# Two edits to a hybrid state-space, attention and feed-forward kernel: B's rows through DRAM with a reordered first group, and a softmax transpose moved to VectorE and the DMA queue

## The chip, the cores and the metric

The kernel runs on one core of a Trainium2 chip, in float32 apart from a few bf16 helpers. The metric is the device time of one execution in microseconds (us). Three runs of the kernel before took 2170.24, 2170.4 and 2171.72 us; the median is 2170.4 us.

A core has five engines that run side by side, each through its own list of instructions in order: TensorE (PE, matrix products, with PEld for its weight loads), VectorE (DVE), ScalarE (ACT), GpSimd (POOL) and SyncE (SP), which here only issues DMAs. They wait for one another through semaphores.

## The reference

The input `x` has shape (16, 256, 128): 16 sequences, 256 tokens, width 128. Four residual blocks follow one another, each on a layer norm of `x`:

```python
x = x + ssm(_layernorm(x), ...)      # selective state space, E = 256 channels, N = 16 states
x = x + ffn(_layernorm(x), ...)      # two layers: windowed attention and a gated MLP
x = x + attn_b(_layernorm(x), W)     # power attention, 16 heads
x = x + ffn(_layernorm(x), ...)      # the same two layers again
```

What matters of the state space block is its recurrence over time, for each of the 16 states:

```python
delta = softplus(xs @ wd1.T @ wd2.T + wd2_b);  Bm = xs @ wb.T;  Cm = xs @ wc.T
h = exp(d_l[:, :, None] * A) * h + (d_l * x_l)[:, :, None] * b_l[:, None, :]
y_l = einsum('ben,bn->be', h, c_l)
```

What matters of a feed-forward layer is its local attention. A sequence has windows of 64 tokens, 8 heads of width 64; a query sees itself and the 64 keys before it:

```python
mask = (i < j) | (i > j + WINDOW) | (j == -1)
attn = softmax(where(mask, -max, einsum('bhwid,bhwjd->bhwij', bq, bk)))
out = einsum('bhwij,bhwjd->bhwid', attn, bv)
```

## The kernel before

**Order.** Each engine is wrapped in `Pinned` (line 78), so that its instructions run in the order in which the program issues them. Every steady loop is written as a list of words: a word is a step, its arguments, and after the colon its lag, the number of iterations by which it runs behind. `wt00.1:4` is the step `wt` for tile 0, half 0, of the second sequence of the group that entered four iterations ago. The order of the words is the order of the instructions on every engine.

**State space block.** The 16 sequences go in 8 groups of 2, so a group has C = 512 columns (2 x 256 tokens), and the 256 channels are 2 halves of 128 partitions. For each group and each of the 16 states n (a "tick") the kernel needs: `decay`, ACT's exponentials; `spread`, a DMA that gives every partition the row of B for state n (tile `bb`); `inputs`, which multiplies delta times x (`dx`) by `bb` into `bx`; `scan`, VectorE's recurrence; `products`, times C, on VectorE or, for three states, on GpSimd; and `add`, TensorE's accumulation. B's rows are computed by `reps`: its weights `wrep` hold each of the 16 columns of B eight times, so the product fills all 128 partitions, `reps_out` copies it to SBUF, and `spread` reads the eight copies of a row and sends each to 16 partitions. The prologue (from `neg_a` and `cw` on) treats group 0 outside the steady list: conv weights `cw`, normed rows, `turn`, convolution into `xe_ps`, `rows`, `reps`, `steps_in`, and then `steps` (delta and dx) and `inputs` for ticks 0 and 1, these on GpSimd.

**Feed-forward blocks.** One runs after the state space block and one after the power block, overlapping it at both ends. A block treats 32 units (2 layers x 16 sequences) as 16 groups of 2, with seven iterations in flight. A sequence is 2 tiles (t = 0, 1) of 128 queries. Per tile: `mask` and `scores` into a pair of PSUM banks, `maxima` and `less_maximum` on VectorE, `exponentials` on ACT, `sums` on VectorE, `weights_of` on GpSimd. This leaves the softmax weights `pr`, 128 queries on partitions by (2 x 4 heads) x 128 keys. The product with V needs keys on the partitions, so `turn_weights` (`wt`) transposes 4 heads at a time on TensorE against the identity, into a PSUM bank, and `turned_weights` (`wc`) copies it to `prT` by ACT. `weigh` (`we`) multiplies V by `prT`. The second tile sees 3 windows of keys and is treated as two halves; in the first tile the queries 0 to 127 see only keys 0 to 127, of which those after the query and those more than 64 before it carry weight 0. `values_out` and `mixed` issue DMAs on SP: two for shifted copies of V, three for the token shift before the MLP. All of a block's tiles lie in one array `mem`, which an `Arena` divides (`FFN_LATE` lists the second part).

**Power block.** It is untouched. Its `spread` reads rows from DRAM (tile `pngd`) and broadcasts them to 128 partitions.

Of the kernel before, what the change touches and what calls it, by code (L numbers as in the profile page):

```python
# [12 lines left out]
F32 = mybir.dt.float32  # L13
# [7 lines left out]
P = 128  # L21
D = 128
L = 256
E = 256
NST = 16
# [20 lines left out]
def kernel(ctx: ExitStack, tc: tile.TileContext, io, out: bass.AP):  # L46
# [72 lines left out]
    def ssm_block(fill):  # L119
        es = ExitStack()  # L120
        w = es.enter_context(tc.tile_pool(name="ssm_w", bufs=1))
        prep = es.enter_context(tc.tile_pool(name="ssm_prep", bufs=1))
        work = es.enter_context(tc.tile_pool(name="ssm_work", bufs=4))
        ps_m = es.enter_context(tc.tile_pool(name="ssm_psm", bufs=1, space=PSUM))
        ps_a = es.enter_context(tc.tile_pool(name="ssm_psa", bufs=1, space=PSUM))
# [23 lines left out]
        wall = w.tile([P, NE, P], F32, name="wall")  # L149

        NR = P // NST
        wrep = w.tile([P, NE, P], F32, name="wrep")
        for e in range(NE):
            part = slice(e * P, (e + 1) * P)
            nc.sync.dma_start(quarters(wall[:, e])[:, :, 0, :], io["wd1T"][part].rearrange("p (j n) -> p j n", j=NQ))
            nc.sync.dma_start(
                quarters(wall[:, e])[:, :, 1, :], io["wcT"][part].unsqueeze(1).to_broadcast([P, NQ, NST])
            )
            nc.sync.dma_start(
                wrep[:, e].rearrange("p (j n) -> p j n", j=NR),  # L160
                io["wbT"][part].unsqueeze(1).to_broadcast([P, NR, NST]),
            )
        wd2T = w.tile([P, E], F32, name="wd2T")
# [119 lines left out]
        def reps(h, q, at=None):  # L283

            q["pb"] = bank([P, C], f"reps_ps_{h}") if at is None else at
            for e in range(NE):
                pe.matmul(q["pb"], wrep[:, e, :], q["xs"][:, e, :], start=(e == 0), stop=(e == NE - 1))

        def reps_out(h, q):
            q["reps"] = prep.tile([P, C], F32, name=f"reps_{h}", tag="reps", bufs=2)  # L290
            act.copy(q["reps"], q.pop("pb"))

# [45 lines left out]

        def steps(h, q, e):
            if e == 0:  # L340
                q["dx"] = prep.tile([P, NE, C], F32, name=f"dx_{h}", tag="dx", bufs=2)
            delta = q["delta"][:, e, :]
            pool.tensor_add(delta, delta, q["av"][:, e, :])
            pool.tensor_mul(q["dx"][:, e, :], delta, q["xs"][:, e, :])

# [5 lines left out]
        def spread(i):  # L351

            bb = live["bb", i] = work.tile([P, C], F32, name=f"bb_{i}", tag="bb")
            src = groups[i // NST]["reps"][i % NST :: NST, :].unsqueeze(1).to_broadcast([NR, NST, C])
            sp.dma_start(bb, src)
# [9 lines left out]

        def inputs(i):
            bx = live["bx", i] = work.tile([P, NE, C], F32, name=f"bx_{i}", tag="bx")
            bb = live.pop(("bb", i)).unsqueeze(1).to_broadcast([P, NE, C])
            pool.tensor_mul(bx, groups[i // NST]["dx"], bb)

# [71 lines left out]
        py = ps_y.tile([P, NE, C], F32, name="cw_ps", tag="y")  # L442
        pts = [py[:, e].rearrange("p (k m) -> p k m", k=DCONV) for e in range(NE)]
        for e in range(NE):
            dve.tensor_tensor(
                tap[:, e], pi[:, e].unsqueeze(1).to_broadcast([P, DCONV, P]),
                conv_w[:, e].unsqueeze(2).to_broadcast([P, DCONV, P]), ALU.mult,
            )
            for k in range(DCONV):
                pe.transpose(pts[e][:, k, :], tap[:, e, k, :], ident)  # L450
            act.copy(cw[:, :, e * P : (e + 1) * P], pts[e])

        sel = w.tile([3 * QW, NST, P], BF16, name="sel")
# [16 lines left out]
        q, r = groups[0], groups[1]  # L470
        normed_rows(0, q)
        turn(0, q)
        turned(0, q)
        more_weights()
# [9 lines left out]
        rows_out(0, q)  # L484
        pb = ps_c.tile([P, C], F32, name="reps_ps_0", tag="c")
        reps(0, q, pb)
# [7 lines left out]
        for e in range(NE):  # L494
            steps_out(0, q, e)
            logs(0, q, e)
            steps(0, q, e)
        for i in range(2):
# [3 lines left out]
        third(0, q)  # L502
        for i in range(2):
            inputs(i)
        rows_of_c(0)
# [36 lines left out]
        for i in range(NG + max(lag for _, _, lag, _ in parts)):  # L542
            for step, more, lag, name in parts:
                h = i - lag
                if (name, h) in done or not (0 <= h < NG or (step is silus and h == NG)):
                    continue
                if step in by_state:
                    step(h * NST + more[0])
                elif step is silus and h == NG:
                    silus(NG, None)  # L550
                elif step is conv:
                    e, half = more
                    conv(h, groups[h], e, range(2 * half, 2 * half + 2))
                else:
                    step(h, groups[h], *more)

                if step is scan and fill is not None and more[0] % 3 == 0:
                    next(fill, None)
# [172 lines left out]

    FFN_LATE = [("rn", 32, 2), ("qkT", 2048, 2), ("vx", 1536, 4), ("pr", 1024, 3), ("prT", 1024, 2), ("oT", 512, 2)]
    FFN_LATE += [("mx", 8, 4), ("rl", 8, 4), ("shifted0", 512, 1), ("shifted1", 512, 1), ("hn", 512, 1)]
# [3 lines left out]
    def ffn_block(k, fw, store, shared):  # L737
# [19 lines left out]
        hTs = [sb.tile([P, L], F32, f"f{k}_hT{i}", f"hT{i}") for i in range(2)]  # L757
        shifted = [sb.tile([P, GT, D], F32, f"f{k}_shifted{i}", f"shifted{i}") for i in range(2)]
        first = []

# [155 lines left out]
        def mask(n, q, t):  # L916
# [4 lines left out]
            if not first:  # L921
# [3 lines left out]
                for h in shifted:  # L925
                    pool.memset(h[:1, 0::2, HD:], 0.0)
            act.copy(
                psim.rearrange("p r h k -> p (r h) k"), fw["bands"][t].unsqueeze(1).to_broadcast([P, 2 * NP, P])
# [49 lines left out]


        def turned_weights(n, q, t, r):  # L980
            if r == 0:
# [3 lines left out]
        def weigh(n, q, t):  # L985

            prT, vx = q.pop(("prT", t)), q["vx"]
            po = bank(q, ("po", t), [P, NP, P], f"f{k}_po_{n}_{t}")
            for p in range(NP):
                for w in range(t + 1):  # L990
                    qs = slice(w * WINDOW, (w + 1) * WINDOW) if t else slice(0, P)
                    for r in range(2):
                        pe.matmul(
                            po[r * DH : (r + 1) * DH, p, qs], vx[:, 2 - w if t else 0, 2 * p + r, :],
                            prT[:, r, p, qs], start=True, stop=True,
                        )
            sb.free(prT)
            sb.free(vx, 2)
# [93 lines left out]
        def unit_sum(g, q):  # L1092
# [12 lines left out]
            nw=newton, no=normed, t=turn, tc=turned, k=mask, s=scores, mx=maxima, lm=less_maximum,  # L1105
            e=exponentials, su=sums, wo=weights_of, wt=turn_weights, wc=turned_weights, we=weigh,
            oc=weighed, mi=mix, ma=mixed, Us=unit_stats, Uf=unit_factors, Un=unit_norm, Ut=unit_turn,
# [3 lines left out]
        period = """  # L1111
            ns.0:0 Uf:5 p00.0:2 e1.1:4 ma0.0:4 ro01.0:2 t11.0:3 s0.0:3 tc11.0:3 ro11.1:3 oc1.0:4
            v0.0:2 sq00.0:2 su1.1:4 ra11.1:3 Ud0:6 vc0.0:2 Un:5 mx0.0:3 t10.0:3 wt00.1:4 ss00.0:2
            tc10.0:3 wt01.1:4 lm0.0:3 wc00.1:4 Ud1:6 ra01.0:2 wc01.1:4 i.1:3 mi1.0:4 n.0:1 wo1.1:4
            p11.0:2 ma1.0:4 Ua:6 v1.0:2 ro00.0:2 nw.1:3 sq11.0:2 k1.0:3 p10.0:2 ss01.0:2 ra00.0:2
            vc1.0:2 p00.1:2 ro11.0:2 Ut:5 no00.1:3 s1.0:3 Uc:5 no01.1:3 e0.0:3 we0.1:4 mx1.0:3
            ra11.0:2 sq10.0:2 nf.1:1 oc0.1:4 ut.0:1 wt10.1:4 ss10.0:2 wt11.1:4 lm1.0:3 wc10.1:4
            Ur10:5 uc.0:1 wc11.1:4 Ur11:5 ss11.0:2 e1.0:3 ro10.0:2 b.0:2 we1.1:4 no11.1:3 k0.1:3
            su0.0:3 ra10.0:2 t00.1:3 oc1.1:4 v0.1:2 tc00.1:3 su1.0:3 no10.1:3 t01.1:3 vc0.1:2
            p01.1:2 sq00.1:2 wo0.0:3 Ur12:5 tc01.1:3 ss00.1:2 sq01.1:2 ro00.1:2 mi0.1:4 i.0:2 Ug:5  # L1120
            wo1.0:3 s0.1:3 ma0.1:4 ro01.1:2 mi1.1:4 nw.0:2 Ur01:5 ma1.1:4 mx0.1:3 ra00.1:2 p10.1:2
            ss01.1:2 t10.1:3 Ub:5 sq10.1:2 Um1:5 t11.1:3 tc10.1:3 v1.1:2 lm0.1:3 tc11.1:3 no00.0:2
            wt00.0:3 vc1.1:2 wt01.0:3 no01.0:2 ss10.1:2 ns.1:0 wc00.0:3 p01.0:1 ro10.1:2 wc01.0:3
            no11.0:2 Ur00:5 k1.1:3 ra01.1:2 wt11.0:3 Um0:5 e0.1:3 wt10.0:3 Us:4 we0.0:3 n.1:1
            ra10.1:2 wc10.0:3 sq01.0:1 s1.1:3 oc0.0:3 su0.1:3 wc11.0:3 ut.1:1 p11.1:2 mx1.1:3
            wo0.1:3 Ur02:5 uc.1:1 Um2:5 t00.0:2 t01.0:2 no10.0:2 tc00.0:2 lm1.1:3 we1.0:3 sq11.1:2
            tc01.0:2 nf.0:0 mi0.0:3 ss11.1:2 k0.0:2 b.1:2
        """
# [436 lines left out]
```

## Time and profile before

| what | us |
|---|---|
| median of the runs | 2170.4 |
| the profiled execution | 2171.14 |
| its span, first to last instruction | 2169.3 |
| TensorE busy | 2028.6 |
| VectorE busy | 1841.5 |
| ScalarE busy | 1706.5 |
| GpSimd busy | 1899.4 |

The span divides into the state space block (to about 490 us), the first feed-forward block (to about 1150), the power block (to about 1500) and the second feed-forward block. The granted TensorE clock is 0.981 on average. A feed-forward block has a pulse: its gate step (three activations and two table loads on ACT, once a group) is at 605.0, 644.9, 684.0, 723.0 us and so on, 39.08 us apart for ten intervals in a row, then 38.87, 30.70 and 25.46 us as it drains; the second block repeats these to 0.1 us. The duration of an instruction in these listings includes its latency; what instructions in a row cost their engine is the distance between their starts.

### The profile page before, as it was taken

Reading aid. Unit: us, or ns where it says so; the run is one execution under the profiler, and the core shown is the slowest. Engines: PE = TensorE matmul, PEld = TensorE weight load, DVE = VectorE, ACT = ScalarE, POOL = GpSimd, SP = SyncE. Lnnn points to the kernel's source line nnn. Section 1 sums busy time; section 2 is a strip of 40 time slices with the busy share of each in tenths; the row PEclk is TensorE's granted clock in tenths of the full one; section 3 lists DMA queues with packets and bytes.
Section 4 is the critical chain, followed back from the end, with each engine's and each line's share of the span. In section 5 each row is a group of like instructions: output and inputs, shape, how many; then the busy total and the mean of one; then the engine's idle time right before and its main releaser. Section 6 shows DMA issues by size and latency. Waiting matters only on the chain.

```text
span 2169.3 us, 44282 instructions
## 1 busy us (share of the span) xinstructions
PE 2028.6 (94%) x16172; PEld 1331.3 (61%) x16174; DVE 1841.5 (85%) x3285; ACT 1706.5 (79%) x2879; POOL 1899.4 (88%) x2183
## 2 busy tenths in 40 slices
PE   5999999877999999999998999998899999999997
PEld 2344444334667777777765777775567777777775
DVE  2999999997989888888856999997988888888873
ACT  4777777746888887887865999997788887878874
POOL 7999999967999888888967999996999988888993
PEclk8999999998999999999997999999999999999998
DMA  4333333321001110111103323230010111101110
GB/s 93 97 83 81 98 80 79 79 52 24 18 22 23 23 23 17 23 23 23 23 11 118 101 98 119 84 114 9 21 23 17 23 23 23 23 16 33 28 28 23
DMA packets 97350, 104.21 MB, mean 48 GB/s; under 512 B 51458, under 2 KB 63596, under 8 KB 97132
## 3 DMA queue, kind: packets, MB, share of 16 engines
q1 hardware_dynamic: 96444, 101.22, 18.4%
q8 instruction: 128, 2.10, 0.4%
q14 instruction: 90, 0.74, 0.1%
q10 hardware_dynamic: 688, 0.15, 0.1%
HBM read 40.28 MB, written 2.36 MB: 20 GB/s over the span
## 4 chain that ended last, share of the span: by engine, by line
PE 54%; POOL 17%; DVE 9%; ACT 9%; issue 7%; DMA 2%; SPq 2%; POOLq 0%; DVEq 0%; ACTq 0%
PE bank L88 44%; POOL bx L88 7%; PE pair L88 7%; POOL mem L88 7%; DVE mem L88 6%; ACT mem L88 5%; DVE hs L88 2%; ACT pair L88 2%; SPq L88 2%; POOL hs L88 1%; PE xe_ps L88 1%; DMA mem<-u_all 1%; DMA bb<-reps 1%; POOL sf L88 1%; PE y_ps L88 1%
## 5 line engine op out<-in xcount | busy, mean ns | idle before, releaser
L88 POOL TENSOR_TENSOR mem<-mem 128x256 f32<-128x256 f32 (+5 forms) x1328 | 1156.7, 901 | 88.4 <-DVE mem L88 66.2
L88 ACT COPY mem<-bank 128x512 f32<-128x512 f32 (+4 forms) x1152 | 590.7, 556 | 147.6 <-PE bank L88 142.0
L88 PEld LDWEIGHTS bank<-ident,mem 128*128 128x128 f32 x3104 | 353.5, 141 | 171.2 <-issue 109.4
L88 PE MATMUL bank<-ident,mem 128*128 128x128 f32 x3104 | 426.0, 277 | 15.1 <-POOL mem L88 10.2
L88 PE MATMUL bank<-wqkv,mem 128*128 128x512 f32 x768 | 385.8, 607 | 1.8 <-ACT mem L88 1.8
L88 DVE TENSOR_REDUCE mem<-mem 128x8 f32<-128x512 f32 (+1 forms) x384 | 325.6, 849 | 9.8 <-ACT mem L88 9.4
L88 DVE TENSOR_TENSOR mem<-bank,rope 128x1024 f32<-128x1024 f32 x256 | 308.8, 1216 | 24.1 <-POOL mem L88 15.8
L88 DVE TENSOR_TENSOR_SCAN hs<-a,bx 128x1024 f32<-128x1024 f32 x128 | 291.4, 2281 | 38.6 <-POOL bx L88 35.5
L88 POOL TENSOR_TENSOR bx<-dx,bb 128x1024 f32<-128x1024 f32 x128 | 298.5, 2357 | 4.0 <-DVE hs L88 3.3
L88 ACT ACTIVATE mem<-mem 128x1024 f32<-128x1024 f32 (+2 forms) x384 | 280.2, 735 | 24.4 <-DVE mem L88 16.3
L88 PE MATMUL pair<-mem 64*64 64x128 f32 (+2 forms) x4096 | 256.7, 296 | 22.0 <-DVE mem L88 13.5
L88 PE MATMUL y_ps<-hs,ident 128*128 128x512 f32 x512 | 242.8, 599 | 11.4 <-DVE hs L88 6.7
L88 PEld LDWEIGHTS pair<-mem 64*64 64x64 f32 (+2 forms) x4096 | 194.9, 160 | 74.2 <-issue 26.2
L88 ACT ACTIVATE a<-delta,neg_a 128x510 f32<-128x510 f32 x256 | 176.0, 689 | 79.1 <-DVE hs L88 73.5
L88 ACT ACTIVATE mem<-bank 128x512 f32<-128x512 f32 (+1 forms) x272 | 160.6, 591 | 62.9 <-PE bank L88 58.6
L88 PE MATMUL bank<-mem 128*64 128x64 f32 (+2 forms) x4608 | 203.3, 255 | 5.3 <-ACT mem L88 2.9
L88 PE MATMUL bank<-mem,w 128*128 128x512 f32 x384 | 193.5, 603 | 3.8 <-ACT mem L88 3.8
L88 PEld LDWEIGHTS bank<-mem 128*64 128x64 f32 (+1 forms) x4608 | 156.8, 128 | 64.3 <-issue 30.1
L88 PEld LDWEIGHTS y_ps<-hs,ident 128*128 128x128 f32 x512 | 95.7, 190 | 154.4 <-issue 125.8
L88 DVE TENSOR_REDUCE mem<-pair 128x8 f32<-128x1024 f32 x128 | 153.2, 1197 | 30.3 <-PE pair L88 29.6
L88 PEld LDWEIGHTS bank<-wqkv,mem 128*128 128x128 f32 x768 | 128.9, 194 | 72.4 <-issue 60.2
L88 DVE TENSOR_TENSOR mem<-pair,mem 128x1024 f32<-128x1024 f32 x128 | 155.5, 1215 | 0.4
(130 smaller groups left out, 2827.0 us busy)
## 6 DMA issues: line engine op xcount, KB each, us to landing
bb<-reps SPq DMA_DIRECT2D x128, 256.0 KB
mem<-pngd SPq DMA_DIRECT2D x64, 512.0 KB
mem<-mem SPq DMA_DIRECT2D x128, 128.0 KB
mem<-u_all SPq DMA_DIRECT2D x64, 64.0 KB
mem<-u_all SPq DMA_DIRECT2D x64, 63.5 KB
x_all<-in_resid_dram SPq DMA_DIRECT2D x8, 256.0 KB
out_dram<-x_all SPq DMA_DIRECT2D x8, 256.0 KB
wqkv<-in_wqkv_dram SPq DMA_DIRECT2D x6, 256.0 KB
```

The source lines that it names most:

```text
L88: bi = getattr(self.eng, name)(*args, **kw)
```

## The change

In the state space block `reps` now makes 16 rows in place of 128. `reps_out` copies them to SBUF and SP writes them to a DRAM tile; `spread` reads one row of it for all 128 partitions. In the prologue a few matmuls of `ident` by `ones` into an unused bank (`warm`) are put between TensorE's first steps, `normed_rows` of group 0 goes ahead of the second `cw` copy, and the `steps` of group 0 and `inputs` of ticks 0 and 1 go to VectorE.

In the feed-forward blocks the first tile's `wt` and `wc` (two of each a sequence) are gone. `blocks_turned` (`bt`) transposes `pr` on VectorE in blocks of 32 by 32, and `blocks_moved` (`bm`) lets SP move nine strips of blocks, each 32 partitions by 1 KB, to the partitions of their keys in a standing tile `y`, one for even and one for odd sequences, set to 0 once. `weigh` reads `y` with a stride. The list `period` is written anew; lags of up to 6 remain.

```diff
-                pe.matmul(q["pb"], wrep[:, e, :], q["xs"][:, e, :], start=(e == 0), stop=(e == NE - 1))
+                pe.matmul(q["pb"], wb[:, e, :], q["xs"][:, e, :], start=(e == 0), stop=(e == NE - 1))
...
-            q["reps"] = prep.tile([P, C], F32, name=f"reps_{h}", tag="reps", bufs=2)
-            act.copy(q["reps"], q.pop("pb"))
+            t = prep.tile([NST, C], F32, name=f"reps_{h}", tag="reps", bufs=2)
+            act.copy(t, q.pop("pb"))
+            q["reps"] = dram.tile([NST, C], F32, name=f"repsd_{h}", tag="repsd")
+            sp.dma_start(q["reps"], t)
...
-            src = groups[i // NST]["reps"][i % NST :: NST, :].unsqueeze(1).to_broadcast([NR, NST, C])
+            src = groups[i // NST]["reps"][i % NST : i % NST + 1, :].to_broadcast([P, C])
             sp.dma_start(bb, src)
...
+        def warm(times):
+
+            for _ in range(times):
+                pe.matmul(warm_bank[:, :L], ident, ones, start=True, stop=True)
+
+        warm(2)
...
+            if e == 1:
+                normed_rows(0, groups[0])
             act.copy(cw[:, :, e * P : (e + 1) * P], pts[e])
+            warm(1)
...
-            steps(0, q, e)
+            steps(0, q, e, dve)
+        inputs(0, dve)
         for i in range(2):
             decay(i)
...
-        for i in range(2):
-            inputs(i)
...
+                if step is scan and (h, *more) == (0, 0):
+                    inputs(1, dve)
...
+                for y in turned_:
+                    pool.memset(y, 0.0)
...
+        def blocks_turned(n, q):
+            x = q["x"] = sb.tile([P, NB, 2 * NP, BS], F32, name=f"f{k}_prx_{n}", tag="prx")
+            pr = q["pr", 0].rearrange("p r h (b k) -> p b (r h) k", k=BS)
+            dve.transpose(x, pr)
+            sb.free(q["pr", 0])
+
+
+        def blocks_moved(n, q):
+            x, y = q.pop("x"), turned_[n % 2]
+            q["y"] = y
+            for i in range(NB):
+                for j in range(max(0, i - WINDOW // BS), i + 1):
+                    sp.dma_start(y[j * BS : (j + 1) * BS, i], x[i * BS : (i + 1) * BS, j])
+            sb.free(x)
...
-            prT, vx = q.pop(("prT", t)), q["vx"]
+            vx = q["vx"]
+            if t == 0:
+                prT = q.pop("y").rearrange("k b (r h) q -> k r h b q", r=2)
+            else:
+                prT = q.pop(("prT", t))
...
-                            prT[:, r, p, qs], start=True, stop=True,
+                            prT[:, r, p] if t == 0 else prT[:, r, p, qs], start=True, stop=True,
```

Of the new period, the words around the new steps, and those of the end:

```diff
+            ns.0:0 we1.0:4 ro01.1:3 bm.1:4 no10.0:3 ut.1:2 ro00.0:2 s0.0:3 b.1:3 uc.1:2 no11.0:3
...
+            ro00.1:2 wo1.0:3 mi0.1:4 Ug:5 bt.0:3 s0.1:3 ra11.0:2 ma0.1:4 bm.0:3 mi1.1:4 mx0.1:3
...
+            no00.0:2 Um2:5 t11.1:3 ns.1:0 we0.0:3 su0.1:3 tc11.0:3 no01.0:2 k1.1:3 v1.0:2 ra11.1:2
...
+            lm1.1:3 t00.0:2 t01.0:2 tc00.0:2 v1.1:2 ss01.1:2 Un:4 sq00.0:1 bt.1:3 tc01.0:2 mi0.0:3
+            k0.0:2
```

The second sequence's `we0.1:4` stands in the first third of the list, as before.

## The prediction, on record before the result

> **What bounds the kernel now.** I first read the busy time of every engine between the gate steps, one pulse of a feed-forward block in each row:
>
> ```profile
> core 0: us, PE busy (x) PEld busy (x) DVE busy (x) ACT busy (x) POOL busy (x), PEclk, DMA share, GB/s
> 605.00:644.90 39.90, 38.71 (x353) 27.53 (x354) 35.21 (x57) 33.04 (x59) 38.26 (x55) 1.00 0.10 21
> 684.00:723.00 39.00, 39.00 (x358) 27.90 (x358) 34.41 (x53) 32.88 (x58) 37.36 (x54) 1.00 0.10 22
> 840.30:879.40 39.10, 39.10 (x362) 28.00 (x360) 33.61 (x49) 31.62 (x55) 33.69 (x45) 1.00 0.10 22
> 1074.60:1105.30 30.70, 30.52 (x329) 23.82 (x328) 24.50 (x38) 25.23 (x40) 29.64 (x37) 1.00 0.09 18
> ```
>
> TensorE fills the pulse; VectorE has 5.5 us free, ACT 7.5, GpSimd 5.4 (in the early pulses, with the norms of the first layer, 1.6). A modelled busy time could hide idle time, so I looked at TensorE's instructions in order of time:
>
> ```profile
> 921.47 1.04 PE L88 MATMUL bank<-ident,mem 128*128 128x128 f32 x8
> 922.34 1.02 PE L88 MATMUL bank<-wqkv,mem 128*128 128x512 f32 x2
> 923.20 1.04 PE L88 MATMUL bank<-ident,mem 128*128 128x128 f32 x8
> 924.07 1.02 PE L88 MATMUL bank<-wqkv,mem 128*128 128x512 f32 x2
> ```
>
> The starts are back to back: eight transposes cost 0.87 us of TensorE, not 8 times their group mean of 277 ns, and a 512-column product 0.86. So a feed-forward pulse is worth what TensorE loses. The state space block is VectorE's: between 108.5 and 162.7 us it is busy 52.78 of 54.20. Its start is a chain I treat separately.
>
> **Feed-forward, what goes.** Per sequence 8 transposes (0.87 us of TensorE) and two ACT copies, which start 0.49 us apart in a run of three that took 1.56. Per pulse: TensorE 1.74, ACT 2.0. That leaves 39.08 - 1.74 = 37.34 us for TensorE. `weigh` does the same matmuls; the strided operand I cost at nothing, since the trace has no such read (below nothing is excluded, as no column goes; the other end is half of the 1.02 us that its 16 records take, 1 us a pulse).
>
> **What comes on VectorE.** Two transposes of 128x1024 a pulse, which no row shows. The nearest rows:
>
> ```profile
> L88 DVE TENSOR_REDUCE mem<-mem 128x8 f32<-128x512 f32 x256 | 172.8, 676 | 7.7 <-ACT mem L88 7.5
> L88 DVE TENSOR_TENSOR mem<-pair,mem 128x1024 f32<-128x1024 f32 x128 | 155.5, 1215 | 0.4
> L88 DVE TENSOR_REDUCE mem<-mem 128x8 f32<-128x1024 f32 x128 | 152.8, 1194 | 2.0 <-ACT mem L88 1.9
> ```
>
> 512 more elements cost 518 ns, so a pass over 1024 costs 1.2 us. Against this stands the Trainium skill, "VectorE: DVE Perf Modes", "The three transpose paths": VectorE turns only 32x32 blocks, 311 ns for a 128x128 bf16 tile against 390 on TensorE, and it sends a full 128x128 turn to TensorE. Eight tiles at 311 are 2.49 us, against 8 x 0.109 here on TensorE. By the page the change buys 0.87 us of TensorE with 2.49 of VectorE a sequence; VectorE would need 33.6 + 5.0 = 38.6 us a pulse, and all but 0.5 of the gain is gone. By the rows it needs 33.6 + 2.4 = 36.0 and fits under 37.34. I take 1.2: a 128-column row here costs 285 ns by itself (u_all<-u_all,bank), nearly the page's 311, so that figure is mostly fixed cost, paid once for 1024 columns. Ends 1.2 and 2.5.
>
> **What comes on SP and the DMA queue.** 18 moves a pulse, each 32 KB from SBUF to SBUF. Here SP's list and the DMA share beside it (the column after PEclk):
>
> ```profile
> 920.26 4.58 SPq L88 DMA_DIRECT2D mem<-u_all  x3
> 924.95 1.20 SPq L88 DMA_DIRECT2D mem<-mem  x2
> 925.00:926.00 1.00, 1.00 0.36 75
> 926.00:927.00 1.00, 1.00 0.76 178
> 927.00:928.00 1.00, 1.00 0.39 90
> 928.00:929.00 1.00, 1.00 0.00 0
> ```
>
> A copy of V costs SP 0.60 us, and the last, issued from about 925.5, is down by 928: 2 to 2.5 us. Nine moves are thus 8 x 0.60 + 2.2 = 7 us from the end of the transpose to the last landing. SP's load rises from 2 x (4.8 + 1.2) = 12 to 22.8 us of a pulse, so it fits. The skill's "DMA: Bandwidth & Descriptors", "Bandwidth", speaks against such moves: under 64 KB they are descriptor-dominated, and one should batch towards 1 MB. In bytes 288 KB at the 178 GB/s above are 1.6 us; by the rule and by SP's row it is the count that costs, 7 us. It is a latency beside TensorE, not in its sum, and it costs nothing only if the list leaves 7 us. I add starts along the new list. TensorE issues `mi0.1` to about 20.2 us after the list's start and reaches `we0.0` at 28.0 (in between: 2 `mi`, 2 scores at 1.0, five projections and rises at 0.86, `ut`, two transposes). VectorE's entries before `bt.0` sum to 18.6, so `x` is ready at 19.8 and the strips at 26.8: 1.2 us spare. For the second sequence `bt.1` ends the list at 36, strips at 43, `we0.1` at 37.3 + 9.1 = 46.4: 3.4 us spare. Behind `bm.0` on SP wait the token-shift DMAs of `ma1.1` and two V copies, behind `bm.1` the V copies of `vc1.1` and the shift of `ma1.0`; their users (`Us`, `we1`) come a good half pulse later. Behind `we0` on TensorE waits everything. ACT loses work. GpSimd gains only the memsets of `y`, two of 0.95 us (the row of a 128x1024 memset), once a block while it fills and GpSimd has 37.4 of 39.1 us: 1 to 2 us a block on the path.
>
> **Sum of a block.** Floors are 37.34 (TensorE), 36.0 (VectorE; 37.0 to 37.6 in the three pulses with norms), 37.4 for GpSimd there. With two engines over 96% I allow 0.25 us a pulse for waits, an estimate; before, VectorE had 5.5 us to absorb them and now 1.3. So 37.6: 1.5 us saved in 8 full pulses, the next of 38.87 and the first draining one of 30.70, 15 us; three early pulses at 1.2, 3.6; the later drain 0.4; the memsets -1.0. That is 18.0 a block, 36.0 for two. The power block is untouched.
>
> **State space block.** The start of group 0:
>
> ```profile
> 13.52 5.79 PE L88 MATMUL xe_ps<-xrT,cw 128*128 128x512 f32 x8 [0.87 <-ACT xrT L88]
> 20.09 3.70 PE L88 MATMUL xe_ps<-xrT,cw 128*128 128x512 f32 x8 [0.78 <-ACT xs L88]
> 32.35 1.26 POOL L88 TENSOR_TENSOR delta<-delta,av 128x512 f32<-128x512 f32 x1 [9.95 <-ACT av L88]
> 37.60 6.96 POOL L88 TENSOR_TENSOR bx<-dx,bb 128x1024 f32<-128x1024 f32 x3
> 31.00:32.00 1.00, 0.00 (x0) 0.00 (x0) 0.00 (x0) 0.97 (x3) 0.00 (x0) 1.00 0.46 98
> 1147.00:1147.50 0.50, 0.47 (x1) 0.30 (x2) 0.00 (x0) 0.50 (x2) 0.16 (x1) 1.00 0.98 401
> ```
>
> The first half of the convolution runs at half clock (0.86 us a record, then 0.43) and takes 5.8 us, the second 3.7. Granted clock fell to 0.50 some 4 us after TensorE stopped at 30 us, and rose 4.6 us after the convolution that starts at 43.65. The `warm` products fill TensorE from about 4.6 us, so the convolution should run fast from its start, near 13: 2.6 us earlier at its end (ends: 0 if the clock rises late, 3). Then delta of half 1, 1.26 us on GpSimd after its queue, is 0.6 on VectorE, which is idle there: the `decay` steps, and behind them on ACT the norm and convolution of group 1, come another 0.8 earlier. Scan 0 (before at 39.97) gains some 5 us, but scan 2, at 52.36, waited for `decay` behind that convolution, and it gains 3.4; from there VectorE is the bound and the 3.4 us stay. B's rows by DRAM move their bytes at 401 GB/s in the power block's row, against 98 on half the engines here; the price is a trip to DRAM of 1.5 us (the power block issues its write at 1141.68, the read at 1143.22). It is hidden: rows near 26, first needed near 33; later groups have `ro` thirty words ahead of `sp0`. In the steady groups GpSimd ran without a break where the chain of waits shows B's DMA, so faster rows save nothing; the upper bound is VectorE's idle 1.4 us a group, 8 us in all.
>
> **Total.** 36.0 + 3.4 = 39.4 us. The profiled execution took 2171.14 us (2169.3 of span and 1.8 around it), which gives 2131.7; the median is 0.7 lower, so 2131.
>
> **Rivals.** (a) VectorE sets the pulse, at 2.0 to 2.5 us a transpose: 38.0 to 39.0 us, 0.1 to 1.1 saved in about 24 pulses, 2140 to 2165. For it: the page's figure, and 36.0 of 37.3 already. Against: the slope of the rows. (b) The strips come late and TensorE waits at `we0`. The spare time is 1.2 and 3.4 us; a chain of 7 us that became 10 (moves at 0.9 us, as the longer issues of the shift suggest, or a queue behind a shift DMA) would stall 1.8 us for the first sequence, as much as the 1.74 gained: from there it is slower. I price it at 11 us: stalls of 2.8 and 0.6 us, less 1.74, over 24 pulses 40 us, with the start 2207. Against: V's copies keep up now at 0.60. (c) The full gain without waits and rows that help: 2 x 21 + 3.4 + up to 8, 2117 to 2125. (d) A copy is moved, but ACT was not the bound, so its 2.0 us give nothing; this holds in all cases.
>
> **Chances.** Forecast with pulses of 37.4 to 37.9: 0.55, own range 2124 to 2140. (a) 0.17, (b) 0.15, (c) 0.10, a wash 0.03. The range 2116 to 2166 takes in (a) and (c) and leaves most of (b) out. One run differs from another by under 0.1%, so 0.2% (4 us) tells a change from none. Faster 0.81, same 0.04, slower 0.15.
>
> **What would show it.** Gate steps 37.4 to 37.9 us apart with TensorE full: right. A VectorE transpose over 2 us, VectorE full and TensorE not: (a). TensorE idle ahead of the 16 records of `we0`, ended by a DMA: (b). Scan 0 near 35 us, the first convolution at 3.7 us and GpSimd idle where `steps` were show the start. A later scan 2 despite that would refute its chain.

## The result and the profile after

The changed kernel takes 2225.62 us, the median of four runs (2224.34 to 2233.31), against 2171.01 us for four runs of the kernel before beside it (2170.24 to 2171.72). The ratio is 1.0259, with a 95% interval of 1.0246 to 1.0271: **54.6 us slower**, where 40 us faster was forecast. The profiled execution took 2224.34 us, its span 2222.6.

The busy time of each engine between gate steps is the table in which the forecast wanted to see 37.6 us a pulse. The columns are the window and its length in us, then busy time and instructions of TensorE, its weight loads, VectorE, ScalarE and GpSimd, the granted clock, the DMA share and GB/s. After the change:

```profile
core 0: us, PE busy (x) PEld busy (x) DVE busy (x) ACT busy (x) POOL busy (x), PEclk, DMA share, GB/s
606.70:648.40 41.70, 38.10 (x342) 25.93 (x342) 37.65 (x60) 31.78 (x54) 37.58 (x53) 1.00 0.14 34
689.40:729.10 39.70, 38.03 (x342) 26.13 (x344) 36.31 (x54) 31.86 (x55) 36.38 (x52) 1.00 0.15 36
886.60:925.80 39.20, 37.92 (x342) 26.02 (x342) 35.56 (x51) 30.04 (x50) 34.26 (x46) 1.00 0.15 36
1083.30:1122.00 38.70, 34.12 (x332) 25.55 (x334) 28.67 (x43) 25.37 (x42) 30.89 (x39) 0.96 0.15 37
```

TensorE's work did shrink, but it no longer fills the pulse: at 886.6 us it is busy 37.92 of 39.20. VectorE, at 35.56, isn't full either. No engine bounds the pulse; waits do. I followed the gate steps through both traces and summed the difference, after minus before: -4.4 us when the state space block ends, +1.7 at the first gate, +8.7 at the thirteenth, +26.4 at the fifteenth, +34.1 at the first gate of the second block, +55.6 at its last. So a full pulse, which was to save 1.5 us, saves nothing. Of the 60 us lost from the end of the state space block on, half lies in the two drains: from the thirteenth to the sixteenth gate the first block takes 94.3 us (before 78.5), the second 89.0 (74.5). Some 14 lie between the first and the thirteenth gates, 16 ahead of the two blocks' first gates.

The clock is not the main reason in the drains. Here the second drain after and before:

```profile
2123.40:2212.40 89.00, 69.61 (x613) 52.45 (x614) 47.25 (x81) 44.01 (x67) 48.55 (x56) 0.92 0.15 37
...
2082.30:2156.80 74.50, 66.10 (x627) 50.97 (x624) 42.00 (x75) 45.87 (x69) 48.56 (x55) 0.92 0.10 24
```

Its granted clock is 0.92 in both, and it is 14.5 us longer. In the first drain the clock is 0.89 against 0.96 and TensorE is busy 5.7 us longer (76.06 against 70.39); by this estimate no more than 5.7 of its 15.8 us are the clock's.

The list of waits of the whole span names those behind the loss. It gives us in total, how often, and the longest:

```profile
DVE mem L88 <- DMA mem<-u_all: 98.8, 32, 6.1
...
PE bank L88 <- DVE mem L88: 54.3, 78, 6.2
...
PE bank L88 <- DMA mem<-mem: 30.6, 19, 5.4
```

Before, the first two were 14.3 us, 9 times, and 16.2 us, 12 times, and the last did not exist. The groups of instructions say which instructions wait (shapes, count, busy us and mean ns, then idle time ahead of them):

```profile
L88 DVE STREAM_TRANSPOSE mem<-mem 128x1024 f32<-128x1024 f32 x64 | 79.2, 1238 | 5.4 <-POOL mem L88 5.0
L88 PE MATMUL bank<-mem 128*64 128x128 f32 x1024 | 76.4, 294 | 54.1 <-DMA mem<-mem 30.6 <-DVE mem L88 17.7 <-ACT mem L88 4.2
L88 DVE BATCH_NORM_STATS2 mem<-mem 128x6 f32<-128x128 f32 x128 | 35.1, 274 | 98.8 <-DMA mem<-u_all 98.8
```

The new transposes cost 1.24 us and hardly wait. The second row is `we0`, which waits for the strips. The third is `Us`, VectorE's statistics of the token-shifted channels: a step that the change did not touch. One pulse in order of time (start, duration, instruction, and in brackets the idle time before it) shows how both come about:

```profile
886.02 1.23 DVE L88 STREAM_TRANSPOSE mem<-mem 128x1024 f32<-128x1024 f32 x1
...
887.32 5.62 SPq L88 DMA_DIRECT2D mem<-mem  x9
...
888.74 0.29 DVE L88 TENSOR_TENSOR u_all<-u_all,bank 128x128 f32<-128x128 f32 x1
...
893.04 4.61 SPq L88 DMA_DIRECT2D mem<-u_all  x3
...
894.33 1.09 PE L88 MATMUL bank<-mem 128*64 128x128 f32 x16 [0.31 <-DVE mem L88]
...
900.20 0.29 DVE L88 BATCH_NORM_STATS2 mem<-mem 128x6 f32<-128x128 f32 x1 [2.78 <-DMA mem<-u_all]
```

The addition of `ma1.1` is done at 889.03, and the three token-shift DMAs could go. On SP they stand behind the nine strips and go at 893.04, **4.0 us late**. By the semaphore events of the trace the last of the three lands at 900.10, 7.1 us after the first was issued; VectorE was ready for it at 897.42 and waits 2.78. The strips are late as well, by less: the ninth is down at 894.24, and `we0` starts at 894.33 after a wait of 0.31. (The bracket names a VectorE instruction; the strip landed after that one had ended, at 894.15.) In each of the 24 pulses between the first and the thirteenth gates `we0` of the first sequence starts 0.1 to 0.5 us after its last strip has landed, and TensorE waits there 0.3 to 1.9 us, 20 us in all. So two waits come from the moves: VectorE's for the shift behind them and TensorE's for the strips.

Why do three small DMAs take 7 us? The first moves 127 partitions. While it is in flight the DMA engines are nearly idle:

```profile
894.40:895.60 1.20, 1.20 (x17) 1.03 (x18) 1.17 (x3) 1.20 (x3) 1.20 (x3) 1.00 0.07 16
```

A share of 0.07 is about one engine in sixteen. The Trainium skill, "DMA: Bandwidth & Descriptors", section "Why a DMA increments its semaphore by 16 and not by 1", says why: the number of engines is the largest up to 16 that divides the outer size, and 127 partitions go to one engine. The trace agrees: the semaphore of this move is updated twice, that of a strip 16 times, and the move takes 6.6 us in every pulse. What is behind it suffers. The next issue on SP, of 0.2 KB, takes 3.08 us; why, no run here shows. Of the third move, of 64 KB, 15 of the 16 updates come by 899.11, 2.2 us after its issue, and the last only at 900.10, after the slow move's end at 899.66.

In a drain VectorE and TensorE wait longer at the same two places; with fewer iterations in flight they have less other work ahead of them:

```profile
1135.01 0.29 DVE L88 BATCH_NORM_STATS2 mem<-mem 128x6 f32<-128x128 f32 x1 [6.05 <-DMA mem<-u_all]
1147.43 1.98 PE L88 MATMUL bank<-mem 128*64 128x128 f32 x16 [5.39 <-DMA mem<-mem]
```

The state space block went as forecast. Its start after the change:

```profile
12.14 3.67 PE L88 MATMUL xe_ps<-xrT,cw 128*128 128x512 f32 x8 [0.44 <-ACT xrT L88]
...
34.23 2.29 DVE L88 TENSOR_TENSOR_SCAN hs<-a,bx 128x1024 f32<-128x1024 f32 x1
...
39.70 5.90 PE L88 MATMUL xe_ps<-xrT,cw 128*128 128x512 f32 x8 [0.78 <-ACT xrT L88]
...
48.22 2.29 DVE L88 TENSOR_TENSOR_SCAN hs<-a,bx 128x1024 f32<-128x1024 f32 x1 [8.18 <-ACT a L88]
```

The first convolution takes 3.67 us where it took 5.79 (the trace's first clock record, of full clock, begins at 10.01 us; before, at 17.79, where the distance of the products fell from 0.86 to 0.43 us). What `warm` does alone was not tried. Scan 0 starts 5.7 us earlier, and scan 2, which waits for ACT behind the convolution of group 1, 4.1 us earlier. From there the gap to the kernel before stays at 4.1 to 4.4 us: the step from the first group's last sum to the second's is 54.37 us (54.30 before), so cheaper rows of B save nothing in the steady groups.

### The profile page after: what moved, and what is told of

Its sections match the earlier page's. It is cut to its first block, busy times and chain, and to the rows that moved or that the text cites. A ratio compares the mean times of both kernels' runs of the same rounds, so it can differ in the third digit from the quotient of the medians.

```text
span 2222.6 us, 43934 instructions
## 1 busy us (share of the span) xinstructions
PE 2004.1 (90%) x15672; PEld 1279.9 (58%) x15672; DVE 1914.6 (86%) x3355; ACT 1661.9 (75%) x2751; POOL 1896.3 (85%) x2181
## 5 line engine op out<-in xcount | busy, mean ns | idle before, releaser
L88 POOL TENSOR_TENSOR mem<-mem 128x256 f32<-128x256 f32 (+4 forms) x1328 | 1158.4, 900 | 87.7 <-DVE mem L88 40.2
L88 ACT COPY mem<-bank 128x512 f32<-128x512 f32 (+3 forms) x1024 | 523.5, 550 | 230.7 <-PE bank L88 223.0
L88 PE MATMUL bank<-wqkv,mem 128*128 128x512 f32 x768 | 398.9, 611 | 6.6 <-DVE mem L88 4.8
L88 PEld LDWEIGHTS bank<-ident,mem 128*128 128x128 f32 x2592 | 298.1, 142 | 164.6 <-issue 109.9
L88 PE MATMUL bank<-ident,mem 128*128 128x128 f32 x2592 | 371.6, 279 | 21.5 <-POOL mem L88 16.6
L88 PE MATMUL pair<-mem 64*64 64x128 f32 (+2 forms) x4096 | 260.9, 301 | 30.3 <-ACT pair L88 16.6
L88 PE MATMUL bank<-mem 128*64 128x64 f32 (+2 forms) x4608 | 209.0, 258 | 55.5 <-DMA mem<-mem 30.6
L88 PEld LDWEIGHTS bank<-mem 128*64 128x64 f32 (+1 forms) x4608 | 162.8, 130 | 131.1 <-DVE mem L88 37.6
L88 PE MATMUL bank<-mem,w 128*128 128x512 f32 x384 | 202.1, 613 | 2.5 <-ACT mem L88 2.5
L88 POOL TENSOR_SCALAR mem<-mem 128x32 f32<-128x32 f32 (+2 forms) x256 | 62.1, 243 | 134.3 <-DVE mem L88 115.9
## 6 DMA issues: line engine op xcount, KB each, us to landing
mem<-u_all SPq DMA_DIRECT2D x64, 63.5 KB
```

What stands on the lines that cost most here:

```text
L88: bi = getattr(self.eng, name)(*args, **kw)
```

## The experiments

My theory after this: what slows the kernel is SP's queue, the moves themselves and what stands behind them. The rivals: the new order of the list is slower whatever it carries; or VectorE's added work is.

**The two edits apart.** Each half of the change was put on the kernel before by itself.

```diff
 ssm_only:  before, with the edits of the state space block
+            q["reps"] = dram.tile([NST, C], F32, name=f"repsd_{h}", tag="repsd")
...
 ffn_only:  before, with the edits of the feed-forward blocks
+            dve.transpose(x, pr)
```

> The state space edits alone, the feed-forward blocks as before. Theory (SP's list): the start gains what the changed kernel's eighth group shows, 4.4 us, so about 2166.6 us, with the gate steps 39.08 us apart as before. Rival (the DRAM trip costs the later groups): over 2169.

> The feed-forward edits alone. If the two parts add up: 2225.6 + 4.4 = 2230 us. If they interact (DMA traffic or the overlap of the blocks), it is more than 3 us away from that.

Measured: 2167.06 us with the state space edits alone (ratio 0.998, 0.9971 to 0.9989), 2234.15 with the feed-forward edits alone (1.0294, 1.0277 to 1.0312). The first is a gain of 4.7 us, the second the whole loss. It is 3 to 4 us more than the two parts need to add up (2234.15 against 2230), just beyond the 3 us that I had allowed for that; this was not traced.

**The moves left out, and the list alone.**

```diff
 no_strips
-                    sp.dma_start(y[j * BS : (j + 1) * BS, i], x[i * BS : (i + 1) * BS, j])
+                    pass
...
 new_list_pe: the first tile turned as before, where bm stands in the new list
-                sp.dma_start(...)
+            for r in range(2):
+                turn_weights(n, q, 0, r)
+                turned_weights(n, q, 0, r)
```

> The changed kernel with the nine DMA moves of each first tile left out (the first tile's weights stay 0, so its attention output is 0). Theory (the moves hold up the token shift on SP and the first tile's product on TensorE): VectorE's wait at the norm statistics falls from 2.8 us a pulse to under 0.5, pulses of 37.3 to 37.9 us, the drains back to about 80 us, in all 2125 to 2140 us. Rival (the new list of steps is slow by itself, or VectorE is full): pulses stay over 38.8 and the drains over 90, 2205 us or more.

> The changed kernel with its new list of steps, but the first tile turned by TensorE and ACT at the place where the moves stand. Theory (the moves, not the list): pulses of 39.0 to 39.3, VectorE's wait at the norm statistics under 0.5 us, drains near 78.5 us as before, in all 2164 to 2178 us. Rival (the list): drains over 90 us and fills longer, 2195 us or more.

Without the moves, which leaves the first tile's attention weights at 0, the kernel takes 2134.23 us (ratio 0.9831, 0.9816 to 0.9845), with pulses of exactly the forecast size and TensorE full:

```profile
862.10:899.70 37.60, 37.60 (x343) 26.16 (x342) 35.84 (x51) 29.77 (x51) 34.96 (x46) 1.00 0.10 23
```

VectorE does all its new transposes here, so they are not the loss; the moves are, with all that follows from them, 91 us. Of these, 46 lie between the first and the thirteenth gates of the two blocks (1.9 us a pulse) and 30 in the drains (5 us a pulse). The same trace shows how much time the list leaves, undisturbed:

```profile
864.74 1.23 DVE L88 STREAM_TRANSPOSE mem<-mem 128x1024 f32<-128x1024 f32 x1
...
867.46 0.29 DVE L88 TENSOR_TENSOR u_all<-u_all,bank 128x128 f32<-128x128 f32 x1
...
872.67 1.09 PE L88 MATMUL bank<-mem 128*64 128x128 f32 x16
...
876.06 0.28 DVE L88 BATCH_NORM_STATS2 mem<-mem 128x6 f32<-128x128 f32 x1
```

From the end of the transpose (865.90, where the next instruction takes over) to `we0` are 6.8 us, and from the end of `ma1.1` (867.75) to the statistic that waits for the shift 8.3. The second of these stretches is 7.2 us in the kernel before, with the shift's DMAs down after 7.1 (at 888.22): it had next to nothing to spare, but there the DMAs went at once:

```profile
880.86 0.29 DVE L88 TENSOR_TENSOR u_all<-u_all,bank 128x128 f32<-128x128 f32 x1 [0.69 <-PE bank L88]
881.18 4.56 SPq L88 DMA_DIRECT2D mem<-u_all  x3
...
888.39 0.27 DVE L88 BATCH_NORM_STATS2 mem<-mem 128x6 f32<-128x128 f32 x1
```

The new list with TensorE's transposes took 2189.08 (1.0082, 1.0067 to 1.0097), 11 us above what I had allowed, with pulses of 39.7 but drains of 79.5 and 77.7. So the order of the list is not what lengthens the drains (80.9 and 73.6 in `ssm_only`). Why its full pulses are 0.6 us longer than before with the same matmuls I did not find; both transposes there stand together at one point of the list.

**The token shift.** One edit moves its users later, the other makes it shorter; two runs combine them.

```diff
 us_late: Us, Uf, Un later in the list
-            ... vc1.0:2 vc0.1:2 Us:4 wo0.1:3 ... mx1.1:3 wt11.0:3 Uf:4 ... ss01.1:2 Un:4 sq00.0:1 bt.1:3 ...
+            ns.0:0 Uf:5 we1.0:4 ro01.1:3 bm.1:4 Un:5 ... sq00.0:1 Us:4 bt.1:3 ...
...
 split_shift: 112 and 15 partitions in place of 127
-                sp.dma_start(h[1:, i : i + 2, HD:], u2[: P - 1, :, HD:])
+                sp.dma_start(h[1:113, i : i + 2, HD:], u2[:112, :, HD:])
+                sp.dma_start(h[113:, i : i + 2, HD:], u2[112 : P - 1, :, HD:])
...
 us_late_split: both;  diag_late_split: both, and in blocks_moved
+            for i in range(NB):
+                part = slice(i * BS, (i + 1) * BS)
+                act.copy(y[part, i], x[part, i])
```

> The changed kernel with the norm statistics of the MLP moved some 4 us later on VectorE's list (and what follows them into the next pulse). Theory A (two waits share the loss: the token shift, queued behind the strips, holds VectorE; the strips' landing holds TensorE): VectorE's wait for the shift goes from 99 us in all to under 25, but TensorE's wait at the first tile's product stays, pulses of 38.0 to 38.8, the drains still over 85 us, 2190 to 2210 us. Rival B (the shift's wait is the whole loss): pulses of 37.6 and about 2145 us.

> The changed kernel with the 127-partition DMA of the token shift cut into one of 112 and one of 15 partitions. Theory A: it ran on one DMA engine and landed 6.6 us after its start, held the next issue on SP for 3.1 us and the last strip's completion on that engine for 1.2 us; so cut, the shift costs SP about 2.7 in place of 4.65 us and lands 3 to 4 us earlier. VectorE's wait falls under 1 us a pulse, TensorE's by about 1, pulses 37.8 to 38.6, drains under 90, 2155 to 2195 us. Rival (only the strips ahead of it count): pulses within 0.3 of 39.3, over 2210 us.

> Both. Theory A: no wait for the shift is left, TensorE's wait at the first tile's product remains as far as the strips take 7 us, pulses of 37.6 to 38.2, 2145 to 2180 us. If the cut alone removed both waits, it equals the run with the cut alone within 5 us.

> Both, and the four strips of nine that stay on their own partitions copied by ACT in place of a DMA: SP's run of strips falls from 5.7 to 3.2 us, ACT gains eight 32x256 copies of about 0.3 us a pulse and has room. Theory A: strips land 2.5 us earlier, TensorE's wait goes, pulses of 37.6 to 37.9, drains near 80, 2135 to 2155 us, faster than the kernel before. Rival (ACT's copies, queued behind the wait for the transpose, hold up its other work): no gain over the run without them, pulses over 38.

Moving the users brought nothing: 2229.11 us (1.0259, 1.0237 to 1.0282), where I had expected 2190 to 2210. Its waits:

```profile
PE bank L88 <- POOL mem L88: 45.5, 46, 6.2
...
PE bank L88 <- DMA mem<-mem: 25.1, 15, 4.0
...
DVE mem L88 <- DMA mem<-u_all: 6.1, 2, 3.2
```

VectorE's wait is gone (98.8 to 6.1 us), and the kernel is no faster. TensorE waits 45.5 us for GpSimd, 16.6 in the changed kernel; the likely step is `Un`, which now stands at the head of the list. With the cut as well it is 2228.21 (1.0256, 1.0223 to 1.0289; expected 2145 to 2180). The moved steps brought waits of their own, so these two runs do not say what VectorE's wait costs. `diag_late_split`, with five strips on SP, took 2176.78 (1.0025, 1.0016 to 1.0033; expected 2135 to 2155). It and `us_late_split` leave VectorE next to no wait for the shift (1.5 us each), and still the shorter strip queue is worth 51 us. In the full pulses of `us_late_split` TensorE waits 23 us for the first sequence's strips, in those of `diag_late_split` not at all. So the strips' own wait counts, beside the shift's.

The cut decides more: 2175.98 us (1.0021, 1.0013 to 1.0028), **50 us less than the changed kernel from one move cut in two**. Its pulse, in order of time:

```profile
761.41 5.63 SPq L88 DMA_DIRECT2D mem<-mem  x9
...
762.85 0.29 DVE L88 TENSOR_TENSOR u_all<-u_all,bank 128x128 f32<-128x128 f32 x1
...
767.15 2.99 SPq L88 DMA_DIRECT2D mem<-u_all  x4
768.45 1.09 PE L88 MATMUL bank<-mem 128*64 128x128 f32 x16 [0.32 <-DMA mem<-mem]
...
771.71 0.29 DVE L88 BATCH_NORM_STATS2 mem<-mem 128x6 f32<-128x128 f32 x1 [0.19 <-DMA mem<-u_all]
```

Four shift DMAs take SP 2.99 us, where three took 4.61, and the last is down 4.4 us after the first was issued. They still start 4.0 us after `ma1.1` (done at 763.14), behind the strips: 4.0 + 4.4 = 8.4 against 8.3 that the list leaves, and VectorE waits 0.19. So nothing is to spare, and in half of the pulses the last landing came only after 4.9 to 6.3 us, so that 29.5 us of this wait are left in the span. TensorE's wait for the first sequence's strips stays, 17 us in the full pulses. In the list of DMA issues the median from issue to landing (last column) of the move of 56 KB is 2.1 us, and the copy of 64 KB behind it also takes 2.1; in the changed kernel that copy took 3.1:

```profile
mem<-u_all SPq DMA_DIRECT2D x64, 64.0 KB, 2.1
mem<-u_all SPq DMA_DIRECT2D x64, 56.0 KB, 2.1
```

**Fewer moves on SP, and the cut elsewhere.** Four of the nine strips stay on their own partitions, so an engine can copy them. ScalarE, which the change relieved, takes them.

```diff
 diag_split: changed kernel, shift cut, and
-                for j in range(max(0, i - WINDOW // BS), i + 1):
+                for j in range(max(0, i - WINDOW // BS), i):
...
+            for i in range(NB):
+                part = slice(i * BS, (i + 1) * BS)
+                act.copy(y[part, i], x[part, i])
...
 diag_split_mid: the same, and
-            ... vc0.1:2 Us:4 wo0.1:3 ... mx1.1:3 wt11.0:3
+            ... vc0.1:2 wo0.1:3 ... mx1.1:3 Us:4 wt11.0:3
...
 ssm_split: ssm_only with the shift cut;  before_split: before with the shift cut
```

> Both edits of the change, with the token-shift move cut into partitions 0 to 111 and 112 to 126, and with four of the nine strips of each group (those that stay on their own partitions) copied by ScalarE, so that SP issues five. Theory: what is left of the loss, once the shift is cut, is the strips' chain. Five moves take 3.0 us on SP instead of 5.4, so the strips land 2.4 us sooner; the full pulses fall from 38.2 to 37.6 to 37.9 us, the time to 2145 to 2165 us, below the state-space edits alone (2167.06). Rival: what is left is the list of VectorE (Us:4 behind ma1.1), which a shorter chain doesn't touch: pulses stay at 38.1 or above and the time at 2170 us or more.

> The kernel with the cut shift and four strips on ScalarE, with Us:4 moved behind mx1.1:3, so that VectorE reads the shifted channels some 1 us later. Theory of the strips: the same time within 0.3% as the kernel without that move. Rival, the shift still holds VectorE: its wait for the shift (29.5 us over the span with the shift cut) goes to under 12 us, and the time falls by 10 us or more against that kernel.

> The state-space edits alone and the shift cut in two; softmax weights of all tiles by TensorE as before. If a move on a single DMA engine costs time only where something stands right ahead of it or behind it in SP's queue, the full pulses stay at 39.1 us and the time at 2162 to 2168 us (2167.06 without the cut). If the slow shift cost the kernel before its time as well, 2150 us or less.

> The kernel before with the shift cut in two and nothing else. In its trace VectorE waits 14.3 us for the shift, 9 times, outside the full pulses. Theory: between no change and 10 us less, 2161 to 2172 us. Rival, that the shift costs every kernel what it costs the changed one: 2130 us or less.

`diag_split` took **2145.79 us** (0.9886, 0.9872 to 0.9899): 24 us faster than the kernel before, the fastest complete version here. TensorE is full again:

```profile
905.00:942.90 37.90, 37.89 (x349) 26.08 (x345) 35.75 (x51) 32.89 (x59) 34.97 (x46) 1.00 0.13 31
```

`diag_split_mid` took 2149.19 (0.9901, 0.9888 to 0.9915), with the same full pulses of 37.9 us: there was no wait for the shift left to remove in them. Its 3.4 us more lie in the drains. The cut helps without the change too: 2163.73 us for the kernel before (0.9971, 0.996 to 0.9981), 2156.49 with the state space edits (0.9936, 0.9923 to 0.9948), 10.6 us under `ssm_only` where I had expected at most 5. The gain comes in the drains, 78.5 to 72.6 and 74.5 to 70.3 us in the kernel before (2.6 us of it are lost again between the two blocks); its full pulses stay at 39.1.

**One cause or two.** The fourth corner of a square (cut or not, nine moves or five), and the floor:

```diff
 diag: diag_split with the shift uncut
 no_strips_split: no_strips with the shift cut
```

> The change with four of the nine strips of each group copied by ScalarE, the shift uncut. It completes a square: both as in the change 2225.6, shift cut 2176.0, shift cut and five moves 2145.8. If the single-engine shift and the number of moves cost each for themselves, the five moves take 30 us off the changed kernel: 2190 to 2200 us, full pulses near 38.9. If the shift is slow only since nine moves stand ahead of it, five are enough: 2145 to 2160 us, full pulses at 38.0. My expectation is between, nearer the first: 2170 to 2195 us, since the shift keeps its 6.6 us but starts 2.4 us sooner, against a wait of 2.76 us in each pulse.

> The moves left out (which leaves out the first tile's softmax weights), with the shift cut: the floor of the new list. Full pulses stay at 37.6 us. If the cut is worth in the drains what it is worth without the change (6 to 11 us), 2123 to 2129 us against 2134.23; then the five moves of the best kernel still cost some 20 us. If the drains do not change, 2134 us and 12 us.

| | nine moves on SP | five | none |
|---|---|---|---|
| shift on one engine | 2225.6 | 2156.1 | 2134.2 |
| shift cut | 2176.0 | 2145.8 | 2127.3 |

`diag` took 2156.13 us (0.9931, 0.9916 to 0.9946), outside the 2170 to 2195 that I had put down and inside the 2145 to 2160 of the other alternative. The costs don't add: the cut is worth 50 us behind nine moves, and only 10 behind five, 7 behind none. Its trace says why:

```profile
909.82 3.10 SPq L88 DMA_DIRECT2D mem<-mem  x5
911.25 0.29 DVE L88 TENSOR_TENSOR u_all<-u_all,bank 128x128 f32<-128x128 f32 x1
...
912.23 1.64 ACT L88 COPY mem<-mem 32x256 f32<-32x256 f32 x4
913.02 4.57 SPq L88 DMA_DIRECT2D mem<-u_all  x3
...
914.59 1.23 DVE L88 TENSOR_TENSOR mem<-bank,rope 128x1024 f32<-128x1024 f32 x1 [1.32 <-ACT mem L88]
...
916.68 1.09 PE L88 MATMUL bank<-mem 128*64 128x128 f32 x16
...
920.91 0.27 DVE L88 BATCH_NORM_STATS2 mem<-mem 128x6 f32<-128x128 f32 x1
```

The shift goes 1.5 us after `ma1.1` (done at 911.54) and needs its 7.0 us as ever: 8.5, against 9.4 until VectorE asks. No wait. For the shift it is a threshold: delay in SP's queue plus time to land, against the time until VectorE asks. With nine moves 4.0 + 7.1 is over the 8.3 by 2.8, and 4.0 + 4.4 stands on it. With five, 1.5 + 7.0 and 1.5 + 4.4 are under 9.4. The 9.4 are 8.3 and 1.1 that VectorE comes later, since it waits 1.32 us for ScalarE, which has the four new copies of strips ahead of its own step; against 8.3 the uncut shift would be 0.2 late. Five moves end the strips' wait too: the fifth is down at 914.21, 2.5 us before `we0`, and in the full pulses of `diag` TensorE does not wait there at all. So going from nine moves to five takes away both waits at once, the cut mainly VectorE's, and the square alone does not divide the loss between them.

`no_strips_split` took 2127.33 (0.9802, 0.9786 to 0.9818), so the five moves and four copies of `diag_split` still cost 18.5 us: 0.3 us a full pulse (the copies hold VectorE up 1.3 us there too; whether that sets the pulse was not tried), and 9 us in the drains, the rest as the pulses fill.

## Why the prediction was wrong

**The step that failed** is the sentence on what is behind the moves: "Behind `bm.0` on SP wait the token-shift DMAs of `ma1.1` and two V copies ...; their users (`Us`, `we1`) come a good half pulse later." That holds for the shift of `ma1.0` (21.5 us in the trace after), not for that of `ma1.1`. There `Us` comes 8.3 us later, under a quarter of a pulse, and the shift's DMAs need 7.0 of these. That left 1.3 us, and the nine moves hold SP for 4.0 us after `ma1.1` is done. VectorE's wait of 2.8 us a pulse, and up to 6 in the drains, follows. The cost of this delay was put at nothing; the cut, which takes most of it away, is worth 50 us. It could be read in the trace of before: the row that I showed of SP's list has three shift DMAs at 4.58 us, against 1.20 for two copies of V, and I asked neither why nor when they are down; and the statistic of `Us` that needs the last of them starts within 0.2 us of its landing.

**The sum of the strips** was right in the chain and wrong in what the list leaves for it. Nine issues at 0.60 and a landing were to be 7 us; they are 7.06 (894.24 less 887.18). From the end of the transpose to `we0.0` I had added up 8.2 us along the list; the undisturbed trace has 6.8. So the 1.2 us to spare were none, and TensorE waits at least 0.3 us in each full pulse, 0.8 on average. This mis-sized term is the second part of the loss. For the second sequence I had 10.4 us where the undisturbed trace has 9.3; its strips were in time in the full pulses.

**What held.** The transpose on VectorE costs 1.24 us, as the slope of its rows gave (1.2), not the 2.5 of the estimate from the 311 ns a tile of the Trainium skill ("VectorE: DVE Perf Modes", "The three transpose paths"); rival (a) is out. TensorE's pulse falls to 37.6 us once nothing waits for moves, so the strided operand costs nothing that can be seen and 0.25 us for waits was the right size. Of the two blocks' forecast 36.0 us, 32.8 came in `no_strips` beside `ssm_only`: 15.9 us between the first and the thirteenth gate of each block, with some 5 us lost again between the blocks, which were not traced. The memsets of `y`, put down at 1 us a block, show no delay in the first block: its first gate comes at 599.5 us in `no_strips`, at 601.4 in `ssm_only`. The state space block gained 4.1 where 3.4 was forecast, by the chain that was named.

**The rivals.** (b) named this side and a queue with the shift DMA, at 0.15 and 2207 us. It put the wait on TensorE, for strips that come late because a move takes 0.9 us or stands behind a shift. Its sign did appear: TensorE idle ahead of `we0`, ended by a strip. But the moves take 0.6 us each, as forecast, and the larger wait is the other way round: the shift comes late behind the strips, for VectorE. The rival did not see that, nor the drains; that it fell only 19 us short is in part luck. The range left it out on the word of V's copies, which keep up at 0.60 us but have nothing behind them that is in a hurry. A step put into a queue is to be priced by what it delays as much as by when it lands itself.

## What to carry to other kernels

When a step puts DMAs on a queue, list for each transfer behind them three numbers from the trace: when it could go, how long it takes from issue to landing, and when its user asks. If the sum of the new issues is over what is left, the cost appears at a step that the change never touched; here it was largest, for one pulse, where the pipeline drains. Look at a transfer that is slow for its bytes before adding to its queue: here cutting one move in two was worth 7 us to the kernel before and 50 to the changed one, and the change with the cut and the shorter queue beats the kernel before by 24 us (2145.8).

## What the runs showed of the hardware

- A move of 127 partitions from SBUF to SBUF (63.5 KB) took 6.6 us and one DMA engine; as 112 and 15 partitions its larger part landed in 2.1 us. It also made the next issue on SP, of 0.2 KB, take 3.1 us; after the cut that issue took 0.6.
- A 128x1024 float32 transpose in 32 by 32 blocks takes VectorE 1.24 us, no more than other passes over 1024 columns in this kernel (1.2).
- In the first draining pulse, where TensorE is busy 34.12 of 38.70 us, the granted clock was 0.96 (1.00 in that pulse before). Over the whole second drain it was 0.92 in both kernels, where the changed one took 14.5 us more.
- A copy of 64 KB issued while the slow move was in flight had 15 of its 16 semaphore updates after 2.2 us and the last after 3.2.
